# Row sums by one wide product, the preparation one slot earlier and last in its slot, in a kNN-convolution and Mamba kernel

## The chip, the core and the metric

The kernel runs on one core of a Trainium2 chip. The metric is device time in microseconds (us), lower is better. Five engines take part, each with its own instruction queue worked off strictly in the order of the program: PE (matrix products), DVE (VectorE), ACT (ScalarE), POOL (GpSimd) and SP, whose queue here does nothing but issue DMAs. An instruction waits on semaphores for what it reads and for the buffer that it writes; everything behind it in its queue waits too.

## The reference, cut to what matters

The input is x, 16 images of 96 channels by 64 by 64, float32. Layer 0 is a graph convolution in 8x8 windows, layer 1 two Mamba blocks and a fusion.

```python
# layer 0, per window of 64 pixels
y    = affine(conv1x1(x, fc1_w, fc1_b), fc1_s, fc1_t)
xn   = nodes / max(norm(nodes), 1e-12)                  # needs a sum over 96 channels per pixel
idx  = top_k(-(distance of xn), 9)
h    = max over the 9 neighbours of gelu((concat(x_i, x_j - x_i) @ ew + eb) * es + et)
x    = affine(conv1x1(h, fc2_w, fc2_b), fc2_s, fc2_t) + x
# layer 1, twice, per image, a sequence of 4096 pixels
h    = (seq - mean) * rsqrt(var + eps) * ln_g + ln_b    # var: a mean over 96 channels per pixel
xs,z = split(h @ in_w);  xc = silu(causal conv of 4 taps over xs)
dt,B,C = split(xc @ xproj_w);  delta = softplus(dt @ dt_w + dt_b)
state = exp(delta * A) * state + delta * B * xc          # a scan over the pixels, 192 x 16 states
seq  = seq + ((sum over states of state * C + D * xc) * silu(z)) @ out_w
# then fusion with a pooled vector, batch norm over all images, and the residual
```

## The kernel before, in words

An image is 8 rows of 512 pixels (8 windows each). An *item* n is one row of one Mamba block of one image: 16 images x 2 blocks x 8 rows = 256 items. Each item has 8 *slots* p, one for each pair of the 16 states, so there are 2048 slots. The 192 channels by two states make three tiles of 128 x 512.

A slot's own work: three decays `da = exp(delta * a)` on ACT (L637), made two slots ahead by `chosen`, which also loads `ct`, the row of C (two DMAs, L633); one product `bt` on PE (L643, `bcast`), which spreads the row of B over the channels, issued one slot ahead; three `db = u * bt` on DVE (L648, `times_b`), of which the first is made a slot ahead, behind the second scan; three scans on DVE (L789); one copy of the end state and one product `hb * ct` on POOL (L802, L803); and the sum over the states on PE (L659 and L661, `folded`), issued one slot later, at the end of that slot's PE work. `bt` has a single PSUM buffer.

All else is *steps*: Python generators, each of which issues a little work and then yields, advanced once per slot between the first scan and the second (at `c == 1`), in the order of the list `going`. They share two PSUM buffers (the pool `pm`, tag "mm"):

- `nearest` (from p = 5 of odd items, one row each): load x, the first convolution, the squares' sum per pixel, reciprocal norms, scores `sc`, and the eight best with DVE's max.
- `edges` (from p = 5 of odd items, the row that `nearest` did two items before): one-hot matrices `oh` on ACT, products `pv`, gathering products `t`, Gelu on ACT, maxima on DVE (the partial calls in `later`, spread between the scans by `between`), the maximum with the node's own term (`hqa`, `hqb`, L455 and L456), and the second convolution `pf` (L462, L465), which DVE adds to x (L474).
- `norm` (inserted at the front of `going` at p = 7, for item n + 3): the variance and `hn`, the normalised row.
- `prelude` (inserted at the front at p = 5, for item n + 2): convolution products `pj` and Silu, `dbl` (dt, B and C), softplus on ACT and POOL, and 16 DMAs that lay `delta` and `u` out over the partitions.
- `tail` (appended at p = 4, for item n - 1): the output product `pow`, added to seq by DVE (L686); for the second block also the fusion product `po`, `o` on ACT and its statistics on DVE (L697).

A step that yields TABLE has loaded another table of activation functions; the decays of that slot are then held back to the end of the next one. `apart(products, use)` issues products at the end of the steps of a slot, and what uses them at the start of the steps of the next. Sums over channels go through `by_pixel` (L271 to L282): four products whose stationary operand is the data, 128 pixels at a time, and whose moving operand is one column of ones, so that 128 pixels' sums land in 128 partitions by 4 columns:

```python
        for j in range(QJ):
            nc.tensor.matmul(ps[:, j : j + 1], lhsT=src.rearrange("c (p j) -> c j p", j=QJ)[:, j, :],
                             rhs=ones_c, start=True, stop=True)
```

In `norm` these sums (tile `pvar`) go by DVE to `v4` (L527), by POOL's power -1/2 (L530) and a round trip through DRAM (L533, L535) to all 96 partitions as `rs`; in `nearest` (tile `ss`) by DVE into `r4` (L314, L315), POOL (L320 to L322) and DRAM to `rn`. Each float32 product shows as two PE instructions in the profile.

Ahead of the 2048 slots a prologue does row 0 to 7 of the first image and the first items' preparation; behind them come the batch norm's end and the output.

Of the kernel before, what the change touches and what calls it, by code (L numbers as in the profile page):

```python
# [20 lines left out]
def tile_conv_knn_mamba(ctx: ExitStack, tc: tile.TileContext, w: dict, out: bass.AP):  # L21
# [12 lines left out]
    WS = 8  # L34
# [95 lines left out]
    srow = load("fc2_srow", [128, C], w["L0_conv_fc2_s"].unsqueeze(0).to_broadcast([128, C]))  # L130
    nc.vector.tensor_tensor(fc2T, fc2T, srow.unsqueeze(1).to_broadcast([128, 3, C]), ALU.mult)
# [23 lines left out]
    ones_c = const.tile([C, 1], F32, name="ones_c")  # L155
    nc.vector.memset(ones_c, 1.0)
# [89 lines left out]
    later = []  # L246
# [23 lines left out]

    def by_pixel(src, name):  # L271

        ps = pm.tile([128, QJ], F32, tag="mm", name=name)
        for j in range(QJ):
            nc.tensor.matmul(  # L275
                ps[:, j : j + 1],
                lhsT=src.rearrange("c (p j) -> c j p", j=QJ)[:, j, :],
                rhs=ones_c,
                start=True,
                stop=True,  # L280
            )
        return ps  # L282
# [5 lines left out]
    def nearest(b, q):  # L288
# [21 lines left out]
        yield  # L310
        r4 = pr.tile([128, 2, QJ], F32, tag="r4", name=f"r4_{nm}")

        def clamped(ps):
            nc.vector.tensor_scalar(r4[:, 0], ps, 1e-24, None, ALU.max)  # L314
            nc.vector.tensor_copy(r4[:, 1], ps)  # L315

        apart(partial(by_pixel, sq, f"ss_{nm}"), clamped)
        yield

        nc.gpsimd.tensor_tensor(r4[:, 0], r4[:, 0], mhalf, ALU.pow)  # L320
# [9 lines left out]
        yield  # L330
# [29 lines left out]
    def edges(b, q):  # L360
# [4 lines left out]


        hqa = pr.tile([128, Q], F32, tag="hqa", name=f"hqa_{nm}", bufs=1)
        hqb = pr.tile([128, QH], F32, tag="hqb", name=f"hqb_{nm}", bufs=1)
        hqa4 = hqa.rearrange("p (r w c) -> p w r c", r=WS, w=NW)
        hqb4 = hqb.rearrange("p (r w c) -> p w r c", r=WS, w=NP)  # L370
        for hf in range(2):
# [5 lines left out]
            yield  # L377
            yield
            vus = []
            for p in range(2):  # L380
                oh = ohs[p]

                ohj = oh[0:NN].rearrange("j w i k -> j w (i k)")
                nc.scalar.activation(ohj, idb[:, 2 * p : 2 * p + 2, :], AF.Abs, bias=minus_node)  # L384
                nc.scalar.activation(ohj, ohj, AF.Relu, bias=1.0, scale=-1.0)

                pv = pm.tile([128, 2, O], F32, tag="mm", name=f"pv_{nm}_{hf}_{p}")
                for h in range(2):
                    nodes = y[:, bass.ts(4 * hf + 2 * p + h, NN)]
                    nc.tensor.matmul(pv[0:NN, h, :], lhsT=nodes, rhs=ew2, start=True, stop=True)  # L390
                    nc.tensor.matmul(pv[NN:128, h, :], lhsT=nodes, rhs=ewd, start=True, stop=True)
                vu = pr.tile([128, 2, O], F32, tag="vu", name=f"vu_{nm}_{hf}_{p}")
                nc.scalar.copy(vu, pv)  # L393
                vus.append(vu)
                yield
            yield


            for p in range(2):
                ohw = [ohs[p][:, h].rearrange("j i k -> j (i k)") for h in range(2)]  # L400
                for part in range(3):
# [12 lines left out]
                    later.append(  # L414
# [36 lines left out]
            if hf == 0:  # L451
                yield
        yield
        yield
        nc.vector.tensor_tensor(hqa, hqa, sa, ALU.max)  # L455
        nc.vector.tensor_tensor(hqb, hqb, sb, ALU.max)  # L456
# [52 lines left out]
    def norm(n):  # L509

        b, i, k = items[n]
        nm = f"{b}_{i}_{k}"
        seq = seqs[b, k]
        hn = hns[n % NHN]
        if k == 0:
            nc.gpsimd.memset(hn[:, :HALO], 0.0)
        else:
            nc.gpsimd.tensor_copy(hn[:, :HALO], hns[(n - 1) % NHN][:, Q:])
        pc = pm.tile([C, Q], F32, tag="mm", name=f"pc_{nm}")
        nc.tensor.matmul(pc, lhsT=cmat, rhs=seq, start=True, stop=True)  # L520
        sq = pr.tile([C, Q], F32, tag="sq", name=f"sqv_{nm}")
        nc.scalar.activation(sq, pc, AF.Square)  # L522
        yield
        v4 = pr.tile([128, QJ], F32, tag="v4", name=f"v4_{nm}")
        apart(
            partial(by_pixel, sq, f"pvar_{nm}"),
            lambda ps: nc.vector.tensor_scalar(v4, ps, 1.0 / C, EPS, ALU.mult, ALU.add),  # L527
        )
        yield
        nc.gpsimd.tensor_tensor(v4, v4, mhalf, ALU.pow)  # L530
        yield
        rs_d = dram.tile([128, QJ], F32, tag="rs_d", name=f"rsd_{nm}")
        nc.sync.dma_start(out=rs_d, in_=v4)  # L533
        rs = pr.tile([C, Q], F32, tag="rs", name=f"rs_{nm}")
        nc.sync.dma_start(out=rs, in_=rs_d.rearrange("p j -> (p j)").unsqueeze(0).to_broadcast([C, Q]))  # L535
        yield
        yield
        nc.gpsimd.tensor_tensor(hn[:C, HALO:], seq, rs, ALU.mult)  # L538

    def prelude(n):  # L540
# [6 lines left out]
        z = pr.tile([128, Q + QH], F32, tag="z", name=f"z_{nm}", bufs=3)  # L547
# [28 lines left out]
        yield  # L576
# [22 lines left out]
        for v, cols in ((va, slice(0, Q)), (vb, slice(Q, Q + QH))):  # L599
            nc.scalar.activation(e[:, cols], v, AF.Abs)  # L600
            nc.scalar.activation(rl[:, cols], v, AF.Relu)
        nc.scalar.activation(e, e, AF.Exp, scale=-1.0)
# [48 lines left out]
    def folded(n, p, hb, y):  # L651
# [3 lines left out]
        if p == 3:  # L655
            nc.tensor.matmul(y[0], lhsT=dp_diag[i][:, 0, :], rhs=xc[:, :Q], start=False, stop=False)
            nc.tensor.matmul(y[1], lhsT=dp_diag[i][:, 1, :], rhs=xc[:, Q:], start=False, stop=False)
        for h in range(2):
            nc.tensor.matmul(y[0][half(h)], lhsT=fold, rhs=hb[:, h, :], start=(p == 0), stop=(p == NPR - 1))  # L659
        for h in range(2):  # L660
            nc.tensor.matmul(  # L661
                y[1][half(h)], lhsT=fold, rhs=hb[:, 2, bass.ts(h, QH)], start=(p == 0), stop=(p == NPR - 1)
            )
# [6 lines left out]
    def tail(n):  # L670
# [17 lines left out]
        if i == NL - 1:  # L688
            yield
            yield  # L690
            yield
            po = pm.tile([C, Q], F32, tag="mm", name=f"po_{nm}")
            nc.tensor.matmul(po, lhsT=fusT[:, 0, :], rhs=seq, start=True, stop=True)
            o = pr.tile([C, Q], F32, tag="o", name=f"o_{nm}", bufs=1)
            nc.scalar.activation(o, po, AF.Identity, bias=gcs[b])
            yield
# [3 lines left out]
    def drain(*several):  # L700

        several = list(several)
        while several:
# [3 lines left out]
            while later:  # L707
                later.pop(0)()
# [8 lines left out]
    for n in range(3):  # L717
        drain(norm(n))
        if n < 2:
            drain(prelude(n))  # L720
# [15 lines left out]
    going = []  # L736
# [4 lines left out]
    for m, (n, p) in enumerate(order):  # L741
# [10 lines left out]
        between.extend(later)  # L752
        later.clear()
        if p == 0 and k == 0:
            state = pr.tile([128, NPR, NB3], F32, tag="state", name=f"state_{nm}")
        if p == 0 and i == 0 and k == 4:
            going.append(pooled(b))
        if p == 7 and n + 3 < NI:
            going.insert(0, norm(n + 3))
        if p == 5 and n + 2 < NI:  # L760
            going.insert(0, prelude(n + 2))
# [7 lines left out]
        for c in range(NB3):  # L769
            if c == 1:  # L770
                if p == 1 and n:
                    gate(n - 1, y)
                if p == 4 and n:
# [5 lines left out]
                still = []  # L779
                for steps in going:  # L780
                    step = next(steps, going)
                    held = held or step is TABLE
                    if step is not going:
                        still.append(steps)
                going = still
# [6 lines left out]
            if between and p not in (0, 1):  # L792
                between.popleft()()  # L793
        if p and behind is not None:
# [65 lines left out]
```

## Time and profile before

| what | us |
|---|---|
| time, median of 3 runs (lowest, highest) | 14857.73 (14852.62, 14866.63) |
| the profiled execution: its time | 14897.12 |
| the profiled execution: its span | 14895.3 |
| PE busy in the span | 13574.3 |
| DVE busy | 13114.8 |
| ACT busy | 10114.4 |
| POOL busy | 10278.8 |
| the slots (496.9 to 14612.0 us): length | 14115.1 |

The page's busy times are unions over the span. PE's matmuls are pipelined and their ends are modelled, so PE's busy time holds time in which it only waits for what is in flight. "PEclk" and the granted clock say which share of full speed PE had; in the records it is either 1.0 or 0.5.

### The profile page before, as it was taken

The numbers are of one execution on the slowest core, as the hardware profiler recorded it, in microseconds if no ns is written. First come the engines' busy times: TensorE is split into PE (matmuls) and PEld (weight loads), VectorE is DVE, ScalarE is ACT, GpSimd is POOL, SyncE is SP. The second block draws the span as 40 slices with busy tenths as digits, with TensorE's granted clock in tenths as the row PEclk, the third lists the DMA queues.
The fourth block names the chain that finished last, engine by engine and source line by source line (L and its number), as shares of the span: only waits on it lengthen the run. The fifth ranks groups of instructions, "written<-read, shape, count | busy, mean of one in ns | idle before, by whom it ended". The sixth has DMA issues, their size and how long they took to land. (4 is left out here: it accounts for less than half of the span.)

```text
span 14895.3 us, 168323 instructions
## 1 busy us (share of the span) xinstructions
PE 13574.3 (91%) x50248; PEld 5491.6 (37%) x50248; DVE 13114.8 (88%) x17401; ACT 10114.4 (68%) x14517; POOL 10278.8 (69%) x6279
## 2 busy tenths in 40 slices
PE   5799999999999999999999999999999999999982
PEld 2233333333333333333333333333333333333330
DVE  2699999999998999999999999999999999999984
ACT  4477777777777777777777777777777677677652
POOL 0577777777777777777777777777777777777771
PEclk8799899989998999999999999999999999989885
DMA  1233333333333333333333333333333333333337
GB/s 27 61 82 86 83 82 83 84 83 81 86 84 79 85 84 83 80 85 85 81 84 84 83 81 86 84 80 85 83 83 82 84 86 80 85 83 82 81 81 218
DMA packets 934023, 1256.95 MB, mean 84 GB/s; under 512 B 304672, under 2 KB 436142, under 8 KB 923888
## 3 DMA queue, kind: packets, MB, share of 16 engines
q1 hardware_dynamic: 929520, 1221.01, 31.7%
q10 hardware_dynamic: 3584, 25.17, 0.4%
q8 instruction: 396, 6.49, 0.2%
q14 instruction: 523, 4.28, 0.1%
HBM read 756.89 MB, written 85.98 MB: 57 GB/s over the span
## 5 line engine op out<-in xcount | busy, mean ns | idle before, releaser
L803 POOL TENSOR_TENSOR hb<-hb,ct 128x1536 f32<-128x1536 f32 x2048 | 7065.1, 3450 | 678.1 <-DVE hb L789 187.2
L789 DVE TENSOR_TENSOR_SCAN hb<-da,state,db 128x512 f32<-128x512 f32 x5376 | 6781.1, 1269 | 0.0
L648 DVE TENSOR_TENSOR db<-u,bt 128x512 f32<-128x512 f32 x6144 | 3992.1, 680 | 672.4 <-PE bt L643 670.3
L637 ACT ACTIVATE da<-delta,a 128x512 f32<-128x512 f32 x6144 | 3900.5, 710 | 61.6 <-DVE hb L789 48.6
L643 PE MATMUL bt<-dbl,bsel 39*128 39x512 f32 x4096 | 2466.0, 683 | 333.6 <-DVE db L648 330.3
L659 PE MATMUL ya<-hb,fold 128*64 128x512 f32 x8192 | 2424.8, 673 | 89.4 <-POOL hb L803 89.1
L802 POOL COPY state<-hb 128x3 f32<-128x3 f32 x1792 | 337.8, 189 | 2975.2 <-DVE hb L789 2550.8
L412 ACT ACTIVATE g<-t,eb,es 128x512 f32<-128x512 f32 x1536 | 1184.8, 777 | 1015.8 <-PE t L404 728.1
L567 ACT ACTIVATE xc<-pj,conv_b 128x512 f32<-128x512 f32 (+1 forms) x512 | 297.4, 581 | 1959.6 <-PE pj L555 1018.8
L661 PE MATMUL yb<-hb,fold 128*64 128x256 f32 x8192 | 1368.8, 415 | 0.0
L404 PE MATMUL t<-oh,vu 128*128 128x512 f32 x2048 | 1176.1, 700 | 45.7 <-ACT vu L393 29.4
L661 PEld LDWEIGHTS yb<-hb,fold 128*64 128x64 f32 x8192 | 640.5, 150 | 1359.0 <-issue 1358.7
L643 PEld LDWEIGHTS bt<-dbl,bsel 39*128 39x128 f32 x4096 | 659.4, 201 | 1164.1 <-DVE db L648 634.7
L555 PE MATMUL pj<-hn,conv_in 97*128 97x512 f32 x2048 | 953.0, 608 | 27.9 <-POOL hn L538 27.9
L789 DVE TENSOR_TENSOR_SCAN hb<-da,db 128x512 f32<-128x512 f32 x768 | 922.6, 1209 | 0.0
L659 PEld LDWEIGHTS ya<-hb,fold 128*64 128x64 f32 x8192 | 503.6, 145 | 1070.4 <-issue 726.9
L407 PE MATMUL t<-oh,vu 128*64 128x512 f32 x2048 | 583.7, 649 | 214.2 <-ACT g L412 209.2
L584 ACT COPY dbl<-pd 38x512 f32<-38x512 f32 x256 | 148.3, 579 | 855.9 <-PE pd L581 855.9
L404 PEld LDWEIGHTS t<-oh,vu 128*128 128x128 f32 x2048 | 386.2, 211 | 801.4 <-issue 521.4
L793 DVE TENSOR_REDUCE hqa<-g 128x64 f32<-128x512 f32 x960 | 634.1, 661 | 0.4 <-ACT g L412 0.3
L390 PE MATMUL pv<-ewT,y 96*64 96x192 f32 x2048 | 478.1, 361 | 124.7 <-ACT sqv L522 124.4
L384 ACT ACTIVATE oh<-idb,minus_node 64x1024 f32<-64x1024 uint16 x512 | 586.9, 1146 | 6.7 <-DMA idb<-idxd 6.7
(160 smaller groups left out, 18671.8 us busy)
## 6 DMA issues: line engine op xcount, KB each, us to landing
ct<-cd SPq DMA_DIRECT2D x4096, 128.0 KB, 3.0
delta<-ln SPq DMA_DIRECT2D x1024, 128.0 KB, 2.4
u<-s SPq DMA_DIRECT2D x1024, 128.0 KB, 2.3
idb<-idxd SPq DMA_DIRECT2D x256, 256.0 KB, 4.0
delta<-ln SPq DMA_DIRECT2D x1024, 64.0 KB, 2.0
u<-s SPq DMA_DIRECT2D x1024, 64.0 KB, 2.0
rs<-rsd SPq DMA_DIRECT2D x256, 192.0 KB, 3.4
x<-in_x SPq DMA_DIRECT2D x128, 192.0 KB, 4.5
```

Source lines behind the costliest of these rows:

```text
L384: nc.scalar.activation(ohj, idb[:, 2 * p : 2 * p + 2, :], AF.Abs, bias=minus_node)
L404: nc.tensor.matmul(t, lhsT=vus[p][:, part, :128], rhs=ohw[part], start=True, stop=True)
L412: nc.scalar.activation(g, t, AF.Gelu, bias=e_b[:, j : j + 1], scale=e_s[:, j : j + 1])
L555: nc.tensor.matmul(ps, lhsT=wt[:, t, :128], rhs=hn[:, off : off + Q], start=(t == 0), stop=(t == taps - 1))
L637: nc.scalar.activation(da, delta[:, c, :], AF.Exp, scale=a_neg[i][:, c, p : p + 1])
L643: nc.tensor.matmul(bt, lhsT=bsel[:, p, :], rhs=made[n][2], start=True, stop=True)
L648: nc.vector.tensor_tensor(db, made[n][5][:, c, :], bt, ALU.mult)
L659: nc.tensor.matmul(y[0][half(h)], lhsT=fold, rhs=hb[:, h, :], start=(p == 0), stop=(p == NPR - 1))
L661: nc.tensor.matmul(y[1][half(h)], lhsT=fold, rhs=hb[:, 2, bass.ts(h, QH)], start=(p == 0), stop=(p == NPR - 1))
L789: nc.vector.tensor_tensor_scan(hb[:, c, :], das[c], dbs[c], state[:, p, c : c + 1] if k else 0.0, ALU.mult, ALU.add)
L793: between.popleft()()
L803: nc.gpsimd.tensor_tensor(hb, hb, ct.unsqueeze(1).to_broadcast([128, NB3, Q]), ALU.mult)
```

## The change

1. `by_pixel` is gone. `norm` makes one product with a 96 x 96 matrix of ones (`ones_cc`), so that the sum stands in all 96 partitions at once, and ACT makes `rs = exp(-0.5 * ln(var + eps))`; `v4`, POOL's power and the DRAM round trip are gone. `nearest` makes one product with one column of ones as stationary operand, a row of 512 sums, which ACT copies and a DRAM round trip spreads to `r4`; the clamp is now on POOL.
2. `norm` starts at p = 0 for item n + 2 (it was p = 7 for n + 3), and takes three steps instead of six. `prelude` starts at p = 4, a slot earlier, in a list `preps` of its own, whose steps come behind those of `going` in each slot; it has no empty step before `dbl`, and a new step boundary in front of the softplus's Exp.
3. `tail` starts at p = 6 (it was 4), with one more empty step between `o` and its statistics; `o` shares the buffer of `xn`; `z` has 4 buffers (3).
4. `edges`: the one-hot matrices of both halves are made a slot earlier in one step; `hqa` and `hqb` are taken later; the maxima (`later`) are issued one slot later; the maximum with the own term goes to a list `late`, issued behind the second scan instead of in front of it; the second convolution `pf` comes two slots later.
5. The products with `dp_diag` open the sum of an item (p = 0) and don't stand in its middle (p = 3).

The short name of the change also has "decays first in a slot"; `ahead()` stands in front of the steps in both versions.

```diff
-    def by_pixel(src, name):
...
@@ nearest
+        ss = pm.tile([1, Q], F32, tag="mm", name=f"ss_{nm}")
+        nc.tensor.matmul(ss, lhsT=ones_cc[:, 0:1], rhs=sq, start=True, stop=True)
+        nc.scalar.copy(sq[0:1], ss)
+        ss_d = dram.tile([1, Q], F32, tag="ss_d", name=f"ssd_{nm}")
+        nc.sync.dma_start(out=ss_d, in_=sq[0:1])
         r4 = pr.tile([128, 2, QJ], F32, tag="r4", name=f"r4_{nm}")
-        def clamped(ps):
-            nc.vector.tensor_scalar(r4[:, 0], ps, 1e-24, None, ALU.max)
-            nc.vector.tensor_copy(r4[:, 1], ps)
-        apart(partial(by_pixel, sq, f"ss_{nm}"), clamped)
-        yield
+        nc.sync.dma_start(out=r4[:, 1], in_=ss_d.rearrange("o (p j) -> (o p) j", j=QJ))
+        yield
+        yield
+        nc.gpsimd.tensor_scalar(r4[:, 0], r4[:, 1], 1e-24, None, ALU.max)
...
@@ edges
             yield
+            for p in range(2):
+                ohj = ohs[p][0:NN].rearrange("j w i k -> j w (i k)")
+                nc.scalar.activation(ohj, idb[:, 2 * p : 2 * p + 2, :], AF.Abs, bias=minus_node)
+                nc.scalar.activation(ohj, ohj, AF.Relu, bias=1.0, scale=-1.0)
             yield
             vus = []
             for p in range(2):
-                oh = ohs[p]
-                ohj = oh[0:NN].rearrange("j w i k -> j w (i k)")
-                nc.scalar.activation(ohj, idb[:, 2 * p : 2 * p + 2, :], AF.Abs, bias=minus_node)
-                nc.scalar.activation(ohj, ohj, AF.Relu, bias=1.0, scale=-1.0)
...
-                    later.append(
+                    later[1].append(
...
-            if hf == 0:
-                yield
-        yield
-        yield
-        nc.vector.tensor_tensor(hqa, hqa, sa, ALU.max)
-        nc.vector.tensor_tensor(hqb, hqb, sb, ALU.max)
+            yield
+        yield
+        late.append(partial(nc.vector.tensor_tensor, hqa, hqa, sa, ALU.max))
+        late.append(partial(nc.vector.tensor_tensor, hqb, hqb, sb, ALU.max))
+        yield
+        yield
         yield
@@ norm
-        v4 = pr.tile([128, QJ], F32, tag="v4", name=f"v4_{nm}")
-        apart(
-            partial(by_pixel, sq, f"pvar_{nm}"),
-            lambda ps: nc.vector.tensor_scalar(v4, ps, 1.0 / C, EPS, ALU.mult, ALU.add),
-        )
-        yield
-        nc.gpsimd.tensor_tensor(v4, v4, mhalf, ALU.pow)
-        yield
-        rs_d = dram.tile([128, QJ], F32, tag="rs_d", name=f"rsd_{nm}")
-        nc.sync.dma_start(out=rs_d, in_=v4)
+        ps = pm.tile([C, Q], F32, tag="mm", name=f"pvar_{nm}")
+        nc.tensor.matmul(ps, lhsT=ones_cc, rhs=sq, start=True, stop=True)
         rs = pr.tile([C, Q], F32, tag="rs", name=f"rs_{nm}")
-        nc.sync.dma_start(out=rs, in_=rs_d.rearrange("p j -> (p j)").unsqueeze(0).to_broadcast([C, Q]))
-        yield
+        nc.scalar.activation(rs, ps, AF.Ln, bias=eps_t[:C], scale=1.0 / C)
+        nc.scalar.activation(rs, rs, AF.Exp, scale=-0.5)
         yield
         nc.gpsimd.tensor_tensor(hn[:C, HALO:], seq, rs, ALU.mult)
...
@@ the slots
-        between.extend(later)
-        later.clear()
+        between.extend(later[0])
+        later = [later[1], []]
...
-        if p == 7 and n + 3 < NI:
-            going.insert(0, norm(n + 3))
-        if p == 5 and n + 2 < NI:
-            going.insert(0, prelude(n + 2))
+        if p == 0 and n + 2 < NI:
+            going.insert(0, norm(n + 2))
+        if p == 4 and n + 2 < NI:
+            preps.append(prelude(n + 2))
...
-                if p == 4 and n:
+                if p == 6 and n:
                     going.append(tail(n - 1))
...
+                for several in (going, preps):
+                    for steps in list(several):
+                        step = next(steps, several)
...
             if between and p not in (0, 1):
                 between.popleft()()
+            while c == 1 and late:
+                late.pop(0)()
```

## The prediction, made before the changed kernel ran

> **What bounds the kernel now.** I read the page first, for the busy engine.
>
> ```profile
> span 14895.3 us, 168323 instructions
> PE 13574.3 (91%) x50248; PEld 5491.6 (37%) x50248; DVE 13114.8 (88%) x17401; ACT 10114.4 (68%) x14517; POOL 10278.8 (69%) x6279
> PEclk8799899989998999999999999999999999989885
> ```
>
> PE's 91% is a union with modelled ends; DVE's 88% is solid work. So I asked for the windows of the stage of the 2048 slots (columns: length, busy of PE, PEld, DVE, ACT, POOL, granted clock, DMA share, GB/s), and for DVE's waits.
>
> ```profile
> 496.90:14612.00 14115.10, 13278.00 (x49252) 5372.91 (x49252) 12914.70 (x17061) 9801.20 (x14180) 10225.54 (x6218) 0.90 0.32 83
> ```
>
> ```profile
> DVE db L648 <- PE bt L643: 670.3, 546, 12.3
> DVE x L474 <- PE pf L465: 314.0, 83, 5.2
> ...
> DVE v L527 <- PE pvar L275: 163.9, 144, 41.3
> DVE r L314 <- PE ss L275: 103.4, 40, 12.8
> DVE stats L697 <- ACT o L695: 102.4, 61, 2.0
> ```
>
> DVE idles 14,115 - 12,915 = 1,200 us of the slots, nearly all waiting for PE: DVE is the bound, PE's lateness the loss. 1,200 us and what DVE work goes is all that can be won. My count of gaps over 0.15 us in the slots alone gives 1,148: db 648, x 298, stats 100, v 89, r 13. They sit in few places: db at p = 2 of even items (345 us, 2.7 each), x at p = 0 of even items (298), db at p = 2 and 3 of odd items (157). One such place, in the timeline of DVE and then of PE:
>
> ```profile
> 8252.75 0.75 DVE L474 SCALAR_TENSOR_TENSOR x<-pf,fc_b,x 96x512 f32<-96x512 f32 x1 [5.10 <-PE pf L465]
> ...
> 8270.46 0.70 DVE L648 TENSOR_TENSOR db<-u,bt 128x512 f32<-128x512 f32 x1 [2.55 <-PE bt L643]
> ```
>
> ```profile
> 8259.03 2.03 PE L275 MATMUL pvar<-ones_c,sqv 96*128 96x1 f32 x8
> 8260.99 1.12 PE L643 MATMUL bt<-dbl,bsel 39*128 39x512 f32 x2
> 8261.95 1.19 PE L593 MATMUL pdta<-dbl,dt_w 39*128 39x512 f32 x2
> 8263.06 1.12 PE L596 MATMUL pdtb<-dbl,dt_w 39*64 39x256 f32 x4
> 8264.46 2.00 PE L275 MATMUL ss<-ones_c,sq 96*128 96x1 f32 x8 [0.28 <-POOL state L802]
> 8266.39 1.98 PE L659 MATMUL ya<-hb,fold 128*64 128x512 f32 x4
> 8268.15 1.07 PE L661 MATMUL yb<-hb,fold 128*64 128x256 f32 x4
> 8269.15 1.28 PE L643 MATMUL bt<-dbl,bsel 39*128 39x512 f32 x2
> ```
>
> Two one-column groups take 4.0 us, and the sum over the states, elsewhere 1.08 + 0.60, takes 1.98 + 1.07: the clock is halved. The windows of slots p = 1 and p = 2 show it (clock 0.80 and 0.74; the next slots 1.00):
>
> ```profile
> 8258.86:8265.31 6.45, 6.15 (x21) 3.78 (x20) 6.39 (x11) 6.42 (x12) 4.63 (x4) 0.80 0.17 46
> 8265.31:8273.44 8.13, 8.11 (x25) 3.44 (x27) 5.58 (x10) 7.60 (x10) 7.49 (x5) 0.74 0.14 24
> ```
>
> What halves it I worked out of all matmul records: streaming time of each product (0.43 us per 512-column instruction at full clock, the spacing in the timeline), times its rows over 128, column halves that run together counted once, summed over each 3.41 us stretch between clock records. Of 345 stretches before a fall the median is 0.19 and 99% lie under 0.35; of 2,946 without a fall 95% lie over 0.35. So one-column groups count nothing, 39-row products 0.3, and p = 1, which holds both, falls.
>
> A page of the Trainium skill speaks against this change: "TensorE: Matmul & The Clock Gate", Part 1, says that the clock halves after an idle window of about 3.4 us. By it one-column products keep PE busy, taking PE work out brings more halving, not less, and only the direct terms below (waits of v, r, stats and the DVE work) would be won, about 390 us. In this trace the clock falls in the middle of the dense queue above, without an idle window, so the trace decides.
>
> **The change, part by part**, against the profiled execution's 14,897 us (median of the runs 14,858, so 39 less).
>
> *One-column products.* 256 + 128 groups of 2.03 us leave PE: 780 us. 256 + 128 wide products come; the nearest row, pc (96 rows, 512 columns), costs 0.93 at full clock (the rate of the pj pairs, 8 in 3.70 us) and 2.02 at half: 357 to 776 us, I take 357. PE is not the bound, so this pays through DVE's waits. Weighted as above, p = 1 gets pvar 0.64, the opening dp_diag products 1.28 and the sum 1.28, and gives pdta, pdtb to p = 7: at least 3.4 of 7.2 us (0.48, odd items), where it was about 1.9 of 6.5 (0.29). Its falls should go. DVE loses v (about 0.1 us each with its gap, 256) and r (0.15, 120): 40 us. Waits v and r: 102 us.
>
> *What replaces them.* ACT: 256 Ln and Exp, nearest rows sqv (579 ns) and da (710): 330 us; 128 copies, nearest row dbl 579: 74. ACT goes from 68% to about 77% of a shorter span; hidden under DVE, except where PE waits for a PSUM buffer that ACT must empty, which I count under the rest. POOL loses 256 powers of 1.02 and gains 128 clamps (0.2 by r's row). SP loses 256 round trips of rs (480 us of SP waiting for rsd) and gains 128 of ss; the write waits for ACT's copy late in p = 1 and the read for the write, holding the ct loads behind them by some 5 us. ct is loaded two slots ahead: hidden; uncovered it would be 5 us x 120.
>
> *The second convolution two slots later.* Its products (2.02 + 1.76 us at half clock) stood behind pc, po, pf, pv, all at half clock, and DVE needed them at once: 5.1 us above. Now p = 1 issues them and DVE wants them 1.2 us into p = 2. I leave 50 of the 298 us. Likewise stats, with one step more behind o: 100 to 0.
>
> *hqa later.* L455 takes 2.04 us in the slots (0.68 in the prologue); it starts at 8234.65 while L803 on POOL runs from 8232.69 to 8236.14, and ends 0.5 us after that. Behind the second scan it starts 1.2 us later, 0.3 before POOL is done: about 0.95 instead of 2.04, times 120 = 130 us (0 if POOL is a slot's third later).
>
> *Preparation a slot up.* Two slots instead of one between u's DMAs and their first use. Its 16 DMAs (SP, 0.6 us each, 10 us) move from p = 4 to p = 3, ahead of the ct loads of p = 4 and 5, used in p = 6 and 7: hidden. *Behind others:* PE does nearest's and edges' products first, prelude's wait for nothing new. *oh in one step:* 4.2 us of ACT at p = 6 behind the decays and ahead of dbl; p = 6 to p = 0 hold some 18 us of ACT against 16.5 to 18 of DVE, made up in p = 1. *Maxima a slot later, tail two later:* the ring of 12 da buffers, z's fourth buffer cover; without them DVE would wait one step, 1 us x 120.
>
> *POOL.* e, ln (2 x 1.8) move to p = 1; ln, s (2 x 1.8) and now hn (1.27) stand in p = 2. With 3.7 of its own per slot POOL has 19.8 us in p = 1 to 3 against 17.9 to 18.5 of DVE. The sum of p = 2, queued in front of the bt that p = 4 needs, then starts at about 0.6 us into p = 4, bt ends near 2.8, needed at 3.5: hidden at full clock, by 0.7 us.
>
> *Prologue.* norm(2) and two DRAM round trips of 6 us or more go, one ss trip comes: -20 (-35 to +30).
>
> *Sum.* Idle DVE: 1,200 to about 350. I keep 200 of db's 648 (a fall at p = 7 to p = 0, where PE has only 0.40 to 0.50 of weighted work, stays possible), 50 of x, 100 for new waits in p = 1 of even items (6.8 to 7.7 us of PE against 6.3 of DVE). 14,897 - 850 - 40 - 130 - 20 = 13,857; less 39: **13,820**. Unknown ends: idle 80 gives 13,550; idle 600 and no gain at hqa 14,200.
>
> **Rivals.**
>
> *A. The clock still falls* at p = 7 and p = 0, now ahead of the densest slot (p = 1 of even items; 15 us at half clock against 6.3 of DVE and 2.5 of slack: 6 us, 120 times = 720). For: a fall from 8242.19 on, after a stretch with no one-column product, in which PE stood 1.47 us. Against: a dense slot fills a stretch with 128-row products, and stretches above 0.65 end most halvings. 13,820 + 400 to 720: 14,220 to 14,540, about 14,380.
>
> *B. Slower: POOL's crowding.* If the sum of p = 2 is over 0.7 us later than I think, PE idles, is halved through the convolution products of p = 4 (3.7 us, 7.4 halved), and p = 4 and 5 each lose: 1.5 us (late bt) and 4 (halved p = 4: 16.2 us to the next bt against 12.1 of DVE), 5.5 per item x 256 = 1,408: 15,230. It decides from 4.1 us per item on (1,040 / 256). Against: PE waits for hb are only 89 us today, and p = 4 and 5 keep 7 us of DVE each.
>
> *C. Nothing moves:* the waits v, x, stats turn into waits for bt, as PE's total stays above 75% of the slots. 14,860. Against: 420 us of PE work are gone at the two slots that halve it.
>
> **How the numbers follow.** Forecast (13,550 to 14,150) 0.67, A 0.18, B 0.09, C 0.03, better than 13,550 0.03. The range 13,560 to 14,450 takes the forecast and most of A, and leaves out B, C, the upper end of A and the lower end (0.2 in all). About 0.2% is what a measurement of this kernel tells from no change: faster 0.88, same 0.03, slower 0.09.
>
> **What would show it.** Right: no v and r among DVE's waits, x after pf under 60 us, db after bt near 200, granted clock in the slots over 0.95, L455 near 1 us, DVE busy over 94% of the slots. A: clock about 0.9, db after bt over 600 with its place at p = 1 or 2 of even items. B: PE waiting long for POOL hb, falls at p = 4. Wrong altogether: DVE idle for ACT or for a DMA.

## The result, and the profile after

The changed kernel takes 15,434.7 us (median of 4 runs, 15,433.2 to 15,439.4) against 14,862.2 (4 runs, 14,852.6 to 14,868.4) for the kernel before: a ratio of 1.0386, 95% interval 1.0368 to 1.0404. It is 572 us slower; the prediction was 13,820, and its range ended at 14,450. In the experiments a time without a range is one execution; the kernel before took 14,852 to 14,873 beside them.

The page after (span; busy time, share and instructions of each engine; granted clock in 40 slices):

```profile
span 15431.4 us, 163022 instructions
...
PE 13454.9 (87%) x47944; PEld 4750.6 (31%) x47944; DVE 12899.1 (84%) x16889; ACT 10507.6 (68%) x15157; POOL 10046.8 (65%) x6151
...
PEclk7789998998989999898998989999898989989885
```

The slots after, in the columns of the slots' window before:

```profile
502.79:15147.63 14644.84, 13148.18 (x47006) 4643.06 (x47005) 12698.98 (x16565) 10191.08 (x14817) 9997.90 (x6087) 0.90 0.29 76
```

DVE's work in the slots fell by 216 us (12,915 to 12,699), more than the 170 forecast (130 for hqa, 40 for v and r). Its idle time rose by 746 instead of falling by 850: 14,645 - 12,699 = 1,946 against 1,200. The sum, +530, is the loss between the two profiled executions, with 6 us more ahead of the slots and under 1 behind them; the medians are 572 apart because the profiled execution of the kernel before, at 14,897, lay 35 us over its median. The waits after (engine, instruction, whom it waited for: us in total, times, longest) say for whom DVE idles, and beside it what ACT and PE wait for:

```profile
DVE db L634 <- PE bt L629: 1466.7, 639, 47.8
...
ACT sqv L516 <- PE pc L514: 1127.9, 254, 6.9
...
POOL e L595 <- ACT s L593: 649.3, 253, 19.1
...
DVE x L468 <- PE pf L459: 524.0, 127, 6.6
...
PE po L678 <- ACT rs L521: 208.1, 60, 3.5
...
PE pdta L578 <- ACT y L290: 156.8, 119, 1.6
...
PE pdta L578 <- ACT scs L338: 146.7, 119, 1.2
```

v and r are gone, stats is down to 3.1 us. But x after pf, forecast at 50, is 524, and db after bt, forecast at 200, is 1,467. Three things are new: the normalisation's square `sqv` waits 1,128 us on ACT, 4.4 per item (16 us in all in the kernel before); PE waits for ACT's logarithm `rs`; and PE waits 306 us in front of `pdta` (1.3 in the kernel before), nearly all of it for ACT to empty a PSUM buffer (the copies `y` and `scs`). POOL's wait for the end of the softplus (s) grew from 129 to 649 us.

My count of DVE's gaps over 0.15 us in the slots (us in all; the first two items and the last are left out; a slot runs from its first scan on DVE to the next one's), and the us per slot in which the granted clock was halved (mean over the items), for the two kernels and four of the experiments below:

| kernel | all gaps | db p=0 | x | db p=2, 3 | halved in p=0 | p=1 | p=2 | p=3 |
|---|---|---|---|---|---|---|---|---|
| before | 1,148 | 36 | 298 (p=0) | 534 | 1.3 | 3.0 | 4.3 | 0.5 |
| after | 1,890 | 724 | 502 (p=2) | 509 | 5.0 | 0.3 | 2.8 | 2.0 |
| softplus in one step | 1,003 | 730 | 24 | 146 | 5.8 | 0.2 | 0.3 | 0.4 |
| after, 128 rows | 1,291 | 340 | 431 | 281 | 1.1 | 0.2 | 3.1 | 0.4 |
| both | 369 | 180 | 6 | 93 | 0.3 | 0.0 | 0.1 | 0.2 |
| before + sums only | 1,708 | 40 | 333 (p=0) | 978 | 1.4 | 1.1 | 3.8 | 3.3 |

So after has two losses: one at p = 0 of nearly every item (240 gaps, 3.0 us each), and one that runs from p = 0 of ACT to p = 2 and 3 of DVE. Both stand in one item's timeline (start, duration, instruction, [idle before, for whom]). ACT, with p = 0 from 8562.91 (first scan on DVE), p = 1 from 8571.37, p = 2 from 8577.61:

```profile
8564.23 0.59 ACT L586 ACTIVATE rl<-pdta 128x512 f32<-128x512 f32 x1
...
8565.24 1.96 ACT L623 ACTIVATE da<-delta,a 128x512 f32<-128x512 f32 x3
8570.87 0.59 ACT L516 ACTIVATE sqv<-pc 96x512 f32<-96x512 f32 x1 [3.67 <-PE pc L514]
...
8572.06 0.85 ACT L588 ACTIVATE e<-e 128x768 f32<-128x768 f32 x1
...
8575.58 1.93 ACT L623 ACTIVATE da<-delta,a 128x512 f32<-128x512 f32 x3
8577.41 0.67 ACT L521 ACTIVATE rs<-pvar,eps_t 96x512 f32<-96x512 f32 x1
```

PE and DVE in the same stretch:

```profile
8562.52 1.12 PE L578 MATMUL pdta<-dbl,dt_w 39*128 39x512 f32 x2 [1.64 <-ACT y L290]
...
8564.15 1.84 PE L645 MATMUL ya<-hb,fold 128*64 128x512 f32 x4
8565.78 1.07 PE L647 MATMUL yb<-hb,fold 128*64 128x256 f32 x4
8566.78 1.58 PE L629 MATMUL bt<-dbl,bsel 39*128 39x512 f32 x2
...
8569.74 1.10 PE L514 MATMUL pc<-x,cmat 96*96 96x512 f32 x2
...
8578.13 2.02 PE L678 MATMUL po<-x,fusT 96*96 96x512 f32 x2 [3.47 <-ACT rs L521]
8579.95 1.75 PE L456 MATMUL pf<-hqa,fc2T 128*96 128x512 f32 x2
```

```profile
8568.40 0.70 DVE L634 TENSOR_TENSOR db<-u,bt 128x512 f32<-128x512 f32 x1 [3.06 <-PE bt L629]
...
8582.60 0.75 DVE L468 SCALAR_TENSOR_TENSOR x<-pf,fc_b,x 96x512 f32<-96x512 f32 x1 [3.71 <-PE pf L459]
```

The clock in two stretches of it (length, busy of PE, granted clock, DMA share, GB/s):

```profile
8564.15:8568.40 4.25, 4.25 (x14) 0.60 0.17 62
...
8577.41:8582.60 5.19, 4.47 (x9) 0.67 0.07 19
```

Read ACT first. The softplus's first half ends at 8565.4; its second half (L588, four instructions, 3.5 us) has its data, but the new step boundary puts it a slot later, and there, behind the other steps, it stands after `sqv`. `sqv` waits 3.67 us for `pc`, which stands on PE behind `bt` and the sum. ACT does nothing in that time, then needs 3.5 us for the softplus and 1.9 for the decays that `ahead` put in front of the slot's steps, and only at 8577.41 reads `pvar`. Until then the two PSUM buffers are taken (`pvar` and `ss`): PE stands 3.47 us at `po`, the clock halves (2.02 and 1.75 us for what takes 1.10 each at full clock), and DVE waits 3.71 us for x. That is the loss at p = 2. The loss at p = 0 is seen above it: `pdta` comes 1.64 us late, for the buffer that `y` empties, then the sum and `bt` run at half clock (1.84 + 1.07 + 1.58 instead of 1.08 + 0.60 + 1.12), and DVE waits 3.06 us. Of these, 1.69 are the half clock's.

### The profile page after: what moved, and what is told of

It reads as the page before. It is cut to its first block, busy times and chain, and to the rows that moved or that the text cites. A ratio compares the mean times of both kernels' runs of the same rounds, so it can differ in the third digit from the quotient of the medians.

```text
span 15431.4 us, 163022 instructions
## 1 busy us (share of the span) xinstructions
PE 13454.9 (87%) x47944; PEld 4750.6 (31%) x47944; DVE 12899.1 (84%) x16889; ACT 10507.6 (68%) x15157; POOL 10046.8 (65%) x6151
## 5 line engine op out<-in xcount | busy, mean ns | idle before, releaser
L645 PE MATMUL ya<-hb,fold 128*64 128x512 f32 x8192 | 2520.9, 697 | 250.7 <-POOL hb L790 249.2
L647 PE MATMUL yb<-hb,fold 128*64 128x256 f32 x8192 | 1430.6, 432 | 0.0
L397 PE MATMUL t<-oh,vu 128*128 128x512 f32 x2048 | 1095.4, 658 | 64.5 <-ACT g L405 51.0
L516 ACT ACTIVATE sqv<-pc 96x512 f32<-96x512 f32 x256 | 151.9, 593 | 1127.9 <-PE pc L514 1127.9
L595 POOL TENSOR_TENSOR e<-e,s 128x768 f32<-128x768 f32 x256 | 465.3, 1818 | 655.3 <-ACT s L593 649.3
L578 PE MATMUL pdta<-dbl,dt_w 39*128 39x512 f32 x512 | 337.3, 744 | 306.0 <-ACT y L290 156.8
```

Source lines behind the costliest of these rows:

```text
L397: nc.tensor.matmul(t, lhsT=vus[p][:, part, :128], rhs=ohw[part], start=True, stop=True)
L647: nc.tensor.matmul(y[1][half(h)], lhsT=fold, rhs=hb[:, 2, bass.ts(h, QH)], start=False, stop=(p == NPR - 1))
```

## The experiments

**The order on ACT.** The theory: ACT's order, not its load, makes x late.

Softplus in one step:

```diff
             nc.scalar.activation(rl[:, cols], v, AF.Relu)
-        yield
         nc.scalar.activation(e, e, AF.Exp, scale=-1.0)
...
         nc.scalar.activation(s1, s1, AF.Identity, bias=neg1)
+        yield
         yield
```

> The changed kernel with the softplus's Exp, +1, Ln, -1 on ACT back in the slot of its Abs and Relu (p = 7, not p = 0); the POOL steps stay where they are. Theory Q: they no longer stand behind the square of the normalisation, which waits for PE at p = 0, so ACT isn't late at p = 1 and 2: x after pf (502 us) under 150, db at p = 3 of odd items (310) under 150, while p = 0 keeps its waits (724) or gets worse by up to 200; 14,800 to 15,100. Theories P and C: within 100 us of 15,435.

Measured: 14,513.0 us, 922 less than after, and 350 less than before; it is a larger gain than expected. ACT's busy time is the same (10,511 against 10,508), its order alone differs. ACT, PE and DVE of the same item:

```profile
8035.42 0.84 ACT L587 ACTIVATE e<-e 128x768 f32<-128x768 f32 x1
...
8043.51 0.59 ACT L516 ACTIVATE sqv<-pc 96x512 f32<-96x512 f32 x1 [2.64 <-PE pc L514]
...
8046.54 0.67 ACT L521 ACTIVATE rs<-pvar,eps_t 96x512 f32<-96x512 f32 x1
```

```profile
8037.51 2.07 PE L629 MATMUL bt<-dbl,bsel 39*128 39x512 f32 x2
...
8047.26 1.10 PE L678 MATMUL po<-x,fusT 96*96 96x512 f32 x2
```

```profile
8039.62 0.69 DVE L634 TENSOR_TENSOR db<-u,bt 128x512 f32<-128x512 f32 x1 [4.16 <-PE bt L629]
...
8050.39 0.75 DVE L468 SCALAR_TENSOR_TENSOR x<-pf,fc_b,x 96x512 f32<-96x512 f32 x1 [0.29 <-PE pf L459]
```

The softplus now runs while ACT waits for `pc` anyway; `rs` comes 3.0 us behind `sqv` (6.5 in the changed kernel), `po` doesn't wait, x waits 0.29. The loss at p = 0 stays (`bt` 2.07 us).

> The changed kernel with the softplus in one step, timed over several rounds. The theory that the step boundary in front of the softplus's Exp is the whole of the loss expects what its single look gave, about 14,513 us and a ratio to the kernel before of about 0.977; a rival, that the single look was luck of one chip, expects a ratio within 0.5% of 1.00.

Measured: 14,504.3 us (14,488.8 to 14,519.6), ratio 0.976, interval 0.9744 to 0.9776.

Preparation first in the slot, the split kept:

```diff
-                for several in (going, preps):
+                for several in (preps, going):
```

> The changed kernel, with the steps of the preparation ahead of the others of their slot again (one line: the list preps is walked before going). Theory Q (queues: ACT works in program order, and the preparation's dbl, softplus and its products stand behind work of the same slot that waits for PE or holds ACT, and PE waits for ACT to empty its two PSUM buffers): the waits of DVE for bt at p = 0 (724 us in the slots of the changed kernel) fall under 250, x after pf (502) under 150, db at p = 3 of odd items (310) under 150; 14,200 to 14,700 us. Theory P (POOL is crowded in p = 1 to 3): POOL has the same work in the same slots, nothing moves by more than 100 us: 15,300 to 15,500. Theory C (too little PE work, so the clock falls more): the same work in each slot, 15,300 to 15,500.

Measured: 14,773.9. x's wait is gone here too, since the second half of the softplus now stands ahead of `sqv`; but DVE waits 400 us more for the scores' copy (m after scs, p = 0 of odd items), behind the preparation on ACT, and the gaps of db at p = 0, expected under 250, stay at 640.

Both edits at once, which tells whether they are one cause:

> The changed kernel with both edits of the first two experiments: the softplus whole at p = 7 and the preparation's steps first. What is left with the softplus whole (14,513 us) is 730 us of waits for bt at p = 0. If the order at p = 7 makes them (the preparation's product pdta queued behind pf and pv, whose PSUM buffers ACT is late to empty), they fall under 250: 13,900 to 14,150. If it is the 4.4 us of one-hot work in ACT's queue at p = 6, ahead of the decays of p = 7 in either order, they stay between 550 and 950: 14,350 to 14,800.

Measured: 14,772.8, no better than the order alone: with the preparation first the boundary no longer matters, and the scores still wait (460 us). For x's wait they are one cause.

The split put into the kernel before (`dbl` a slot earlier there, so that the steps stay in place):

```diff
         nc.scalar.preload_act_table_set("natural_log_exp_and_others")
         yield
-        yield
         dbl = dbls[n % 2]
...
             nc.scalar.activation(rl[:, cols], v, AF.Relu)
+        yield
         nc.scalar.activation(e, e, AF.Exp, scale=-1.0)
```

> The kernel before with only the preparation's new step boundaries: dbl a slot earlier (p = 7, no empty step), products and Abs and Relu at p = 0, Exp, +1, Ln, -1 at p = 1; POOL and DMA steps stay. There the preparation is first in its slot, so nothing of the old order is turned around; ACT gets 1.9 us less at p = 1 and 2.5 more at p = 7 and 0. Theory Q: the waits for bt at p = 2 and 3 (502 us) fall under 250, x after pf at p = 0 (298) stays or grows by 100: 14,550 to 14,800. If splitting the softplus costs by itself, as undoing it won 922 us in the changed kernel: 15,200 to 15,800.

Measured: 15,043.5, some 180 slower, between the two times expected. The boundary costs in both orders, five times as much in the new one: it is the boundary together with the preparation's place behind the other steps that costs 922 us.

More ACT work alone: three useless activations (1.5 us per item) in `norm` of the kernel before, whose results nobody reads.

```diff
+        nc.scalar.activation(spare, spare, AF.Ln)
+        nc.scalar.activation(spare, spare, AF.Exp)
+        nc.scalar.activation(spare, spare, AF.Identity)
         v4 = pr.tile([128, QJ], F32, tag="v4", name=f"v4_{nm}")
```

> The kernel before with three activations more per item on ACT (Ln, Exp and a copy of 96 x 400 numbers in SBUF that nothing reads, about 1.4 us), in norm's step of p = 0, behind the decays. They wait for nothing and nothing waits for their result. If ACT's queue is the limit there, whatever it works on: the waits for bt at p = 2 and 3 (502 us) grow by 300 to 600, as with the new row sums (15,394): 15,150 to 15,450. If ACT has room (68% busy): within 100 us of 14,858.

Measured: 14,872.0 (14,863.7 for the kernel before beside it), no change, though ACT is busy 380 us more (10,494 against 10,114). The next wait behind them took the work up: that of `dbl` for its product is 431 us in all, against 856 in the kernel before.

**The one-hot matrices.** Halves apart again, each ahead of its own products (the edit in short):

```diff
-            for p in range(2):
-                ohj = ... ; Abs ; Relu
             yield
             vus = []
             for p in range(2):
+                ohj = ... ; Abs ; Relu
```

> The changed kernel with the one-hot matrices made again one half at a time, right ahead of their products (p = 7 and p = 0, as before the change), not both at p = 6. Theory Q, if the 4.4 us block at p = 6 in front of dbl is what makes ACT late at p = 7: the waits for bt at p = 0 (724 us) fall to 200 to 450 and with them x and odd p = 3 (812 together) to under 600: 14,700 to 15,150. If it is only the order of the preparation that counts, and not the block: within 150 of 15,435. Theories P and C: the same, within 150 of 15,435.

Measured: 15,878.5, 444 slower than after, which no theory expected. The copies `vu` stand behind `oh` on ACT and hold a PSUM buffer each: x's gaps grow from 502 to 822. Making `oh` in one step, which I had suspected, helps in this order.

`oh` a slot earlier still (`edges` from p = 4, one more empty step behind `oh`), with the softplus in one step:

> The changed kernel with the softplus whole at p = 7 and the one-hot matrices one slot earlier, at p = 5 (edges starts at p = 4, with an empty step after them, so that its products stay in their slots). If the one-hot block ahead of dbl and of the decays of p = 7 makes the waits of p = 0 (730 us with the softplus whole), they fall under 250; at p = 5 the block now stands ahead of three Silus, for which PE's two buffers wait: 50 to 300 us of new waits at p = 5 and 6. 13,850 to 14,250. If the block doesn't matter: 14,400 to 14,650.

Measured: 15,060.0, 547 slower than the softplus alone. The gaps of p = 0 go (730 to 88 us), but p = 6 loses 920; the waits name the new place.

```profile
PE pj L547 <- ACT xc L554: 865.1, 240, 6.9
ACT oh L367 <- DMA idb<-idxd: 768.6, 245, 9.8
```

`oh` stands ahead of the Silus and waits for its DMA. With the preparation first in all slots of that kernel, and in p = 4 to 6 only:

```diff
-                for several in (going, preps):
+                for several in ((preps, going) if p in (4, 5, 6) else (going, preps)):
```

> The same as the run before in this call, with the preparation's steps first in their slot, so that the Silus of p = 5 and the softplus of p = 7 stand ahead of the one-hot block and of y and scs. If ACT's order is the whole matter: waits of DVE in the slots under 400 us in all, 13,700 to 13,950, below both kernels. If POOL's crowding (p = 1 to 3) or the clock holds it: over 14,200, with PE waiting for POOL's hb ahead of DVE's waits.

> The changed kernel with the softplus whole at p = 7, the one-hot matrices at p = 5, and the preparation's steps first at p = 4, 5 and 6 (Silus and dbl ahead of the one-hot block) but last elsewhere (pf, y, sc and scs ahead of the softplus at p = 7). Theory Q: neither the waits of p = 0 (730 us with the softplus whole, 770 as db with 460 to 500 of scs when the preparation is first at p = 7) nor those of p = 6 (920 us when the one-hot block stands ahead of the Silus) are left: under 350 us of DVE waits in the slots, 13,600 to 13,950. If the DMA that brings the indices makes the one-hot block late at p = 5 whatever stands ahead of it: 200 to 500 us of waits at p = 6 and 7, 14,000 to 14,300. Theory P (POOL): over 14,200, with DVE's waits at p = 3 and 4.

Measured: 14,883.6 and 14,459.6. In the first the scores wait again (499 us). In the second p = 6 is cured and p = 0 is back (634 us), with `oh` in the same early place: so it wasn't `oh` that held PE up at p = 0, and the 88 us probably came of DVE being late already. Of the orders on ACT that I tried, this is the best, far from the 13,600 to 13,950 that theory Q expected.

**The row sums.** The new sums alone in the kernel before (one wide product, ACT's Ln and Exp; `ss` likewise):

> The kernel before with the row sums alone changed (one wide product, Ln and Exp on ACT, in nearest the row of sums by way of DRAM), every step in its old slot and order. Theory Q: the sums are not what costs; v, r go (102 us), the waits for bt at p = 2 of even items (345 us) fall under 120, the clock in the slots rises from 0.90 to 0.93 or more, x after pf stays near 300: 14,300 to 14,600. Theory C: PE has less work, so the clock falls as much as before or more: 14,750 to 15,100. Theory P says nothing of it.

Measured: 15,394.0, some 530 slower, where both theories expected less. The halving at p = 1 falls from 3.0 to 1.1 us per slot, as the prediction said it would, and DVE's gaps rise by 560, mostly at p = 2 and 3. One place in PE's timeline there:

```profile
8551.11 1.87 PE L300 MATMUL ss<-sq,ones_cc 96*1 96x512 f32 x2 [1.78 <-ACT rl L585]
```

`ss` waits for a PSUM buffer that the softplus's Relu still holds, and its copy on ACT stands behind the rest of the softplus. To see whether the wait within one slot is all of it, the products at the end of a slot and ACT's part at the start of the next, by `apart`:

> The kernel before with the row sums alone changed (15,394 us in the first call), but with their products at the end of a slot and ACT's Ln and Exp (and the copy of the row) at the start of the next, where the old kernel had DVE read the one-column sums. If the loss of 533 us comes from ACT waiting for the sum's product in the same slot, with dbl, one-hot and copies behind it: 14,500 to 14,950. If ACT is simply full between p = 0 and p = 2, so that 1.3 us more of Ln and Exp make the Gelus of p = 2 late wherever they stand: 15,150 to 15,500, with the waits for bt at p = 2 and 3 as in the first call (about 980 us).

Measured: 15,278.1, only 116 of the 530 back. What the rest is in the old order stays open. In the new order, the old one-column sums of `norm`, started a slot earlier, with the softplus in one step:

> The changed kernel with the softplus whole (14,513 us), and in norm the one-column products, v4 on DVE, the power on POOL and the DRAM round trip again (norm starts at p = 7 for item n + 3, and its hn comes at p = 3, not 2). Theory Q, with ACT near its limit between p = 0 and p = 2: 330 us of ACT work are gone and the waits for bt at p = 0 and 2 shrink by 100 to 400 us: 14,100 to 14,450. My prediction's reason (one-column products beside 39-row products halve the clock, and that is what costs): clock half in a larger share than 0.17, waits at p = 1 to 3 grow by 100 to 500: 14,600 to 15,000.

Measured: 14,606.8, 94 more than with the wide sums: 24 of them ahead of the slots, where the norm of a third item is made, 31 of DVE's own work (`v4`), and some 40 of waiting. The clock is halved at p = 1 again (3.2 us per slot against 0.3), but that costs little here. So the wide sum of `norm` pays a little in the new order; in the old one the wide sums cost 530.

**The clock at p = 0.** The theory (R in the expectations): 39-row products count too little for the clock, and at p = 7 and p = 0 they stand together (pdta, pdtb, bt). The test fills `dbl`, `dt_w` and `bsel` with zeros to 128 rows: as many instructions as before, of the same length at full clock.

```diff
-    bsel = const.tile([R + 2 * NS + 1, NPR, 128], F32, name="bsel")
+    bsel = const.tile([128, NPR, 128], F32, name="bsel")
+    nc.vector.memset(bsel, 0.0)
...
-        t = const.tile([R + 2 * NS + 1, Q], F32, name=f"dbl{i}")
-        nc.vector.memset(t, 1.0)
+        t = const.tile([128, Q], F32, name=f"dbl{i}")
+        nc.vector.memset(t, 0.0)
+        nc.vector.memset(t[: R + 2 * NS + 1], 1.0)
...
-            dw = const.tile([R + 2 * NS + 1, D], F32, name=f"dt_w{i}")
+            dw = const.tile([128, D], F32, name=f"dt_w{i}")
...
```

In the kernel before, in the changed one, with the softplus in one step, and in the version with the order by slots:

> The kernel before with dbl, dt_w and bsel held in 128 rows, zeros below row 38: the products bt, pdta and pdtb go over 128 rows and not 39, with the same columns, count and order of instructions. Theory R (the clock halves when the products' time, weighted by their rows, is under about 0.35 of a 3.41 us stretch): bt counts 0.85 us and not 0.26 in every slot; the share of halved clock falls from 0.22 to under 0.10, the waits for bt at p = 2 of even items (345 us) under 120, x after pf at p = 0 (298) under 150: 14,100 to 14,450. If zeros or rows don't count, or the halving only follows from waiting: share 0.20 to 0.23, 14,830 to 14,890.

> The changed kernel with the same 128-row products. Theory R with theory Q: the halving at p = 7 and 0 goes (share of halved clock 0.22 to under 0.10), with it most of the waits for bt at p = 0 (724 us to under 250); ACT then waits less for the squares' product at p = 0, so that x after pf (502) and p = 3 of odd items (310) shrink by half or more: 14,000 to 14,600. Theory Q alone (ACT's order is the cause, the halving a consequence): 15,300 to 15,450, share 0.20 or more.

> The changed kernel with the softplus whole at p = 7 (14,513 us) and the 128-row products. Theory R: the 730 us of waits at p = 0 fall under 200, halved clock under 0.06: 13,750 to 14,000, below both kernels. Theory Q alone: within 60 us of 14,513.

> The kernel with the softplus whole, the one-hot block at p = 5 and the preparation first at p = 4 to 6 (14,460 us), and the 128-row products. Theory R: the 634 us of waits at p = 0 fall under 150 and little else is left: 13,700 to 13,950. Theory Q alone: within 60 us of 14,460.

Measured: 14,750.9 (some 110 less than before), 14,819.2 (616 less than after), 13,876.6 (636 less than without the padding), 13,866.8 (593 less). Mean granted clock over the span: 0.891 to 0.929, 0.893 to 0.931, 0.915 to 0.970, and 0.913 to 0.969. The first two are short of what theory R expected (14,100 to 14,450 and 14,000 to 14,600): the kernel before keeps its one-column groups, the changed one ACT's order (431 us of gaps at x). The last two are within it. PE's wait in front of `pdta` hardly changes (306 us in the changed kernel, 301 with the zeros; 272 and 247 with the softplus in one step), while the halving at p = 0 nearly goes (5.0 to 1.1 and 5.8 to 0.3 us per slot): so it is the halving, and not that wait, that costs most at p = 0. The two repairs add up: 922 + 616 = 1,538, together 15,434.7 - 13,876.6 = 1,558. Timed:

> The changed kernel with the softplus in one step and the 39-row products padded with zeros to 128 rows, timed over several rounds. The two causes together (ACT's queue and the halved clock of the narrow products) expect about 13,877 us, a ratio to the kernel before of about 0.934, under 0.94; the rival, that padding merely gained from one chip's clock, expects a ratio close to that of the kernel without padding, 0.977.

Measured: 13,878.4 us (13,864.8 to 13,887.0), ratio 0.9333, interval 0.9317 to 0.9348: faster than both kernels. Its slots' window, the `bt` of the same place and the `db` behind it (the latter two in the version's single execution):

```profile
507.47:13597.42 13089.95, 11914.58 (x47013) 4431.15 (x47012) 12673.91 (x16564) 10152.03 (x14817) 9991.55 (x6087) 0.99 0.33 85
```

```profile
7674.25 1.12 PE L631 MATMUL bt<-dbl,bsel 128*128 128x512 f32 x2
...
7675.41 0.69 DVE L636 TENSOR_TENSOR db<-u,bt 128x512 f32<-128x512 f32 x1 [0.43 <-PE bt L631]
```

DVE is busy 12,674 of 13,090 us (97%) at a clock of 0.99, idle 416.

## Why the prediction was wrong

**The step that failed first** is one that the part-by-part account doesn't have. The new step boundary in front of the softplus's Exp, with the preparation last in its slot, stands in the diff, and no term prices it on ACT. ACT's new work was "hidden under DVE, except where PE waits for a PSUM buffer that ACT must empty", and for such waits the sum holds 100 us, worked out of PE's load in p = 1 of even items. "Behind others" had PE's order looked at and ACT's not; even for PE its "prelude's wait for nothing new" is wrong, since `pdta` waits 306 us. Loads were summed (18 us of ACT against 16.5 to 18), where the order decides: ACT stood idle 3.67 us at `sqv` with 3.5 us of ready work behind it, and x waited 502 us where 50 were left for it. Undoing the boundary is worth 922 us.

**The second is the place of the halved clock**, in "I keep 200 of db's 648". The weighing itself held: p = 1 lost its falls (3.0 to 0.3 us per slot), and raising the weight of the 39-row products by zeros alone takes 593 to 636 us out of the new order. But the change moved pdta and pdtb to p = 7 and p = 0; the prediction gave that place 0.40 to 0.50 of weighted work, called a fall there possible, and kept 200 us for all of db. The fall is the rule there: 5.0 us per slot at p = 0, and 724 us of gaps.

**Rival A** had this half: the place of the falls (p = 7 to p = 0). It named another victim, p = 1 of even items, 120 times 6 us; DVE lost the time at p = 0 itself, behind the sum and `bt`, 240 times 3.0 us, so that its 720 comes so near is luck. With the boundary undone the kernel takes 14,504 us, within A's 14,220 to 14,540. **Rival B** was right in sign and wrong in mechanism: it put 1,408 us of loss at p = 4 and 5, where the gaps are 146 and the clock is halved for 0.5 us per slot; PE's waits for POOL's hb rose only from 89 to 249 us; and with the softplus in one step, which leaves POOL's order as it is, 922 us come back. **Rival C** is out: the time moved by 4%, and what DVE waits for is two places, not PE's total.

**What held**: v and r gone from DVE's waits, stats 100 to 3; `hqa` with 0.66 us instead of 1.91 won 159 us (130 forecast); DVE's work fell by 216. "I leave 50 of the 298" for x and the 350 us of idle DVE are nearly met once both causes are gone: 6 us of gaps at x, 416 us idle, 13,878 us against the 13,820 forecast. The zero rows are no part of the change, so this doesn't make the sum right; it shows that no third loss of this size was left out. The prologue's -20 was +6. The sum was a sum of gains under a condition, that ACT and the clock stay out of the way, and the condition had no number.

**The clock's rule.** I redid the prediction's weighting on the matmul records of both kernels' slots, in stretches of 3.41 us at full clock, each product's streaming counted from its recorded start. In the kernel before, 95% of 355 stretches ahead of a fall weigh under 0.35 (the prediction had 99%; the median is 0.20, the heaviest 0.49), and none of the 2,969 others does. In the changed kernel only 72% of 429 do, and of the 213 that lead to a fall in p = 7 or p = 0 half, up to 0.51; the lightest without a fall weighs 0.36. So the weight sorts, but between 0.36 and 0.51 it tells nothing, and the 0.40 to 0.50 that the prediction found for this place lay there. In the kernel before, 67% of the falls follow a stretch in which PE, by the profile's modelled ends, was never idle, and 1% an idle time of 3.4 us or more; in the changed kernel every fall follows some idle time and 33% one of 3.4 or more, but of those in p = 7 and p = 0 none over 1.72. Padding 39 rows to 128 with zeros cut the share of time at half clock from 0.170 to 0.060 with the softplus in one step and from 0.215 to 0.138 in the changed kernel, at the same instruction count. The Trainium skill, "TensorE: Matmul & The Clock Gate", Part 1, ties the lower clock to an idle window of about 3.4 us; zeros fill no idle time, and most falls here need no such window, so an idle window alone can't explain these runs, and the measurement decides. "PSUM — Partial Sum Buffer", section "Engine vs sequencer instructions", says that ScalarE's queue is strictly first in, first out: that agrees with the 3.67 us of idle ACT above, and is the rule that I should have held against the new order.

## What to carry to other kernels

For each instruction that is moved, list what stands in front of it and behind it on its own engine, and ask what the one in front waits for; an engine that is busy 68% of the time can still cost 900 us when ready work queues behind a wait. Price every new step boundary, even one that adds no work. Where PE's clock is in play, look for the stretch in which narrow products gather, and try zero rows: here they cost no time of their own, and brought some 600 us in the new order (with the softplus in one step a clock of 0.970 instead of 0.915), but only some 110 in the kernel before.

## What the runs showed of the hardware

- The granted clock follows the rows that a product uses, zeros included: `bt` takes 1.12 us with 39 or 128 rows at full clock, but with 128 rows in bt, pdta and pdtb the falls in a run (softplus in one step) drop from 274 to 101.
- The same 128 rows in the kernel before win only about 110 us (clock 0.929): p = 1, with its one-column groups, still has 1.7 us per slot at half clock (3.0 without the padding). Neither the wide sums nor the rows bring the full clock alone.
- An engine's idle time could be filled for nothing where its next wait took the work up: 380 us of added ACT work moved the time by less than 0.2%, and the wait behind it fell by 425 us.
